# Two ways of turning matrices and of taking a norm's statistics in a graph-network kernel: DMA transposes against 32x32 blocks on VectorE, and bn_stats against two summing passes on ScalarE

## The chip, the cores and the metric

The kernel runs on one core of a Trainium2 chip. The metric is the device time of one execution in microseconds (us), lower is better; where several runs were made, their median is given. All data are 32-bit floats.

## What is computed

The input `x` holds 128 graphs (batch) of 128 nodes with 512 features; `adj` is one 128x128 adjacency matrix that all graphs share. Two residual layers follow each other, each with a layer norm and a relu ahead of it:

```python
# layer 0: graph convolution
h = max(layernorm(x), 0)
deg = adj.sum(axis=1);  d = where(deg > 0, rsqrt(deg), 0)
norm_adj = adj * d[:, None] * d[None, :]
x = x + norm_adj @ (h @ W0) + b0
# layer 1: attention over the graph's edges, 8 heads of 64
h = max(layernorm(x), 0)
q, k, v = h @ Wq + bq, h @ Wk + bk, h @ Wv + bv
scores = q k^T / 8 + (1 - adj) * -1e9
x = x + (softmax(scores) v) @ Wo + bo
```

## The kernel before, in words

**Groups and slots.** The 128 graphs are worked in 32 groups `g` of four (`GB = 4`; graphs b = 0 to 3 of a group, in two halves of two). The work is software-pipelined over time steps `t`, and the order on every engine is the order of the program text: nothing is reordered afterwards. One time step runs five blocks on TensorE: W (the graph convolution's product of group t+1), Q, K and V (the three projections of group t) and Y (the output projection of group t-1). `block` (L1108) runs each as seven steps. Around each step it calls what `plan` has put at a place: the place "Q2" stands ahead of the dense work of step 2 of block Q (`step`, L523), "Q2b" between that and the reads that belong to it (`rest`, L612), "Q2c" behind those. `at(t, place, f, ...)` (L926) fills the plan; the loop from L929 on holds all of it, written out by hand. On one engine an instruction that waits holds up all behind it.

**The products.** From group 1 on each 512-deep product is made by a Winograd-like scheme of seven products (P1 to P7, L31), some of which are split once more in the same way. The operands of the left side lie in a tile of 40 slots of 128 columns (`Operands`, L362: `op_mix` for the convolution, `op_norm` for the normalised and turned h of the attention, `op_att` for the attention's output). Its sums and differences are made by `combine` (L378), mostly on GpSimd. For Q and K the weights are the stationary operand and `op_norm` the moving one (`stay`); for V, W and Y it is the other way round. `halves` (L137) issues each matmul as two of 64 stationary columns. TensorE's results go to PSUM banks a0, a1, b, c, d0, d1; ScalarE makes the first read of a region with the bias (`first`, L785), VectorE adds the later ones (L448, L463). A bank is written again only when its reads are done. In step 1 the product P5 goes to d0 and d1; ScalarE's and VectorE's reads of it stand in `rest` of steps 1 and 2; in step 4 P3 is accumulated onto d1 and then d0. Except in K, the last two pieces of P4 are put off into `tail` and run within steps 1 and 2 of the next block (`left`, L527).

**The turned matrices.** Two things have to be transposed: h ahead of Q, K and V, and the 128x128 attention matrices of the eight heads of each graph (`att`, 128x1024) ahead of `attend` (L890), which stands at V0. For most groups that goes through DRAM. ScalarE splits the 32-bit words into two planes of 16 bits (`split_h` L753, `split_att` L872), the planes are written to DRAM (`write_h` L759, and within `split_att`), and a transposing DMA, which works on 16-bit words here, brings them back turned and interleaved (`turn_h` L762, `turn_att` L878). Groups 0, 1 and 31 have h transposed on TensorE instead (`transpose_h`, as bf16 halves of the words, L742), and some attention matrices at the two ends are too (`turned_in_place` L817, `transpose_att` L881). Five buffers `att_buf` rotate: the turned matrix of graph b lands in the buffer of b-1.

**The norms.** `Norm.statistics` (L331) runs bn_stats and bn_aggr on VectorE for each graph; `scale` (L335) makes 1/sqrt(var + eps) and the negated mean times that on GpSimd; `normalised` (L344) applies both with a relu on ScalarE. The first norm of group t+2 (`ln1`) stands at Q0b, Q1b (half 0) and Q3b (half 1); it is applied (`gcn_norm`) at Q3, Q4, Q5b, Q6 and multiplied with the adjacency matrix on TensorE (`gcn_mix`, tile `pa`) at Q5, Q6, K1, K2. The second norm (`ln2`) of group t+1 stands at K0b and K6b.

**Queues.** All DMAs are issued on SP's queue in program order: reloads of the weights in five parts (`reload_w` L1077), the loads of x two groups ahead, the stores, the planes and the transposing DMAs.

Where the tail is taken up, in `step`:

```python
left = tail.pop(0) if n in (1, 2) and tail else None
...
elif n == 1:
    if inner:
        self.seven(P5, True, (0,))
    ...
    if left:
        left[0]()
    if inner:
        self.seven(P5, True, (1,))
```

Of the kernel before, what the change touches and what calls it, by code (L numbers as in the profile page):

```python
# [8 lines left out]
F32 = mybir.dt.float32  # L9
# [76 lines left out]
def combine_one(engine, t, left, pair, step):  # L86


    def twice(n):
        x, y = (slot_of(left, k, n) for k in pair)  # L90
        return t[:, x : y + 1 : y - x, :]

    out, x, y, minus = step
    engine.tensor_tensor(twice(out), twice(x), twice(y), ALU.subtract if minus else ALU.add)  # L94
# [3 lines left out]
def kernel(  # L98
# [34 lines left out]
    sp = ctx.enter_context(tc.tile_pool(name="sp", bufs=6))  # L133
# [3 lines left out]
    def halves(out, lhsT, rhs, **flags):  # L137

        for y in range(0, P, P // 2):
            nc.tensor.matmul(out[y : y + P // 2], lhsT[:, y : y + P // 2], rhs, **flags)  # L140
# [16 lines left out]
    planes_dram = [dp.tile([P, 2, H * P], U16, tag=f"planes_{b}", name=f"planes_{b}") for b in range(GB)]  # L157
    h_dram = [dp.tile([P, 2, H * P], U16, tag=f"planes_h_{y}", name=f"planes_h_{y}") for y in range(2)]
# [25 lines left out]
    class Weight:  # L184
# [6 lines left out]
        def slot(self, k, n):  # L191
            return self.t[:, slot_of(False, k, n), :]

# [41 lines left out]
    ident16 = const.tile([P, P], BF16, name="ident16")  # L235
# [4 lines left out]
    warm = const.tile([P, 1], F32, name="warm")  # L240

    def constants():
# [5 lines left out]
        nc.gpsimd.tensor_copy(ident16, ident)  # L248
# [41 lines left out]
    def combine_inner(name, engine, steps=range(9)):  # L290
        for k in steps:
            pair, step = INNER[k]
            combine_one(engine, w_sb[name].t, False, pair, step)
# [26 lines left out]
    class Norm:  # L320


        def __init__(self, src, name):
            self.src = src
# [6 lines left out]
        def statistics(self, j):  # L331
            nc.vector.bn_stats(self.st[:, j, :], self.src[:, j, :])
            nc.vector.bn_aggr(self.mv[:, j, :], self.st[:, j, :])

        def scale(self, js):  # L335
            c = slice(js[0], js[-1] + 1)
            nc.gpsimd.tensor_scalar(self.ve[:, c], self.mv[:, c, 1], EPS, None, ALU.add)
            nc.gpsimd.tensor_tensor(self.rs[:, c], self.ve[:, c], mhalf[:, c], ALU.pow)
            for j in js:
# [22 lines left out]
    class Operands:  # L362
        def __init__(self, name):
            self.t = op.tile([P, SLOTS, P], F32, tag=name, name=name)

        def blocks(self, i):
            return self.t[:, LEFT_AT[i] : LEFT_AT[i] + 4, :].rearrange("p (c j) n -> p c j n", c=2)

        def slot(self, i, n):
            return self.t[:, slot_of(True, i, n), :]  # L370

        def blocks_of(self, b):
# [3 lines left out]
            return self.t[:, first + j : first + 8 : 2, :]  # L376

        def combine(self, engine, inner=True, then=None, within=None):  # L378
# [6 lines left out]
            if inner:  # L385
                for step in FIRST_LEFT:
                    combine_one(within, self.t, True, (S1, S4), step)
                for step in WINOGRAD_LEFT:
                    combine_one(within, self.t, True, (A12, A22), step)


    op_mix, op_norm, op_att = (Operands(f"op_{k}") for k in "aho")
    tail = []

    class Projection:
# [13 lines left out]
        def product(self, out, product, fresh):  # L409
# [3 lines left out]
            left, right = self.left.blocks(i), self.right.blocks(k)  # L413
            for c in range(2):
                for r in range(2):
                    start = fresh and c == 0 and r == 0
                    if self.stay:
                        self.matmul(out[:, r], left[:, c], right[:, c, r * P : (r + 1) * P], start)
                    else:
                        self.matmul(out[:, r], left[:, c, r, :], right[:, c, :], start)  # L420
# [224 lines left out]
    def ln1(g, half, js=(0, 1), ready=None):  # L645

        if (g, half) not in scale1:
            scale1[g, half] = Norm(source(g, half), f"1_{g}_{half}")
# [9 lines left out]
    def gcn_mix(g, b):  # L658
# [7 lines left out]
        src = pa.rearrange("p (c n) -> p c n", c=NC)  # L666
        if g == 1 and b < 2:
            nc.vector.tensor_copy(op_a[g].blocks_of(b), src)
        else:
            nc.scalar.copy(op_a[g].blocks_of(b), src)  # L670
# [60 lines left out]
    def transpose_h(g, b):  # L731
# [5 lines left out]
        planes = pt.bitcast(BF16).rearrange("p (z c n) -> p z c n", z=2, c=NC)  # L737
        words = h2.bitcast(BF16).rearrange("n (c f z) -> n z c f", c=NC, z=2)
        for z in range(2):
            for c in range(NC):  # L740
                for y in range(0, P, P // 2):
# [520 lines left out]
```

## Time and profile before

| What | Value |
|---|---|
| median of 3 runs | 2200.97 us (2200.22 to 2202.0) |
| the profiled execution | 2200.75 us, its span from first to last instruction 2199.0 us |
| granted TensorE clock | 0.999 |
| DMA | 595.48 MB, 271 GB/s; its hardware queue's packets took 90.6% of 16 engines' span |
| packets under 512 B | 389,073 of 530,613 |
| transposing DMAs | 121 for att, 58 for h |
| splitting on ScalarE | L875: 121 of 1894 ns; L757: 116 of 1055 ns |
| statistics on VectorE | L332: 144 of 673 ns and 112 of 677 ns; L333: 256 of 182 ns |
| time from issue to landing, median | att planes written 6.3 us, h planes written 3.2 us |

PE is TensorE's matmul row, PEld its weight loads, DVE VectorE, ACT ScalarE, POOL GpSimd, SP the queue that issues the DMAs. In a row of instruction groups there stand the line, the engine, the operation, output and inputs by the program's names, the shapes and the count; then the busy time in us and the mean of one in ns; then the idle time just ahead of them and what ended it. In a timeline the first column is the start in us, the second the length of a run of like instructions, and the bracket at the end gives the idle time ahead and its releaser. In the table by stretch there stand the stretch, its length, the busy time of PE, PEld, DVE, ACT and POOL with their instruction counts, the granted clock, the DMA engines' share and GB/s. A 32-bit matmul appears as two records.

### The profile page before, as it was taken

The numbers are of one execution on the slowest core, as the hardware profiler recorded it, in microseconds if no ns is written. First come the engines' busy times: TensorE is split into PE (matmuls) and PEld (weight loads), VectorE is DVE, ScalarE is ACT, GpSimd is POOL, SyncE is SP. The second block draws the span as 40 slices with busy tenths as digits, with TensorE's granted clock in tenths as the row PEclk, the third lists the DMA queues.
The fourth block names the chain that finished last, engine by engine and source line by source line (L and its number), as shares of the span: only waits on it lengthen the run. The fifth ranks groups of instructions, "written<-read, shape, count | busy, mean of one in ns | idle before, by whom it ended". The sixth has DMA issues, their size and how long they took to land.

```text
span 2199.0 us, 77713 instructions
## 1 busy us (share of the span) xinstructions
PE 2186.2 (99%) x31749; PEld 1879.6 (85%) x31749; DVE 1774.9 (81%) x4244; ACT 1393.8 (63%) x3604; POOL 1886.1 (86%) x2049
## 2 busy tenths in 40 slices
PE   9999999999999999999999999999999999999999
PEld 7788888888888888888888888888888888888887
DVE  7777888878888778888788887788877888878876
ACT  4577665765666666666656676566666565765654
POOL 7988988898889898888988898888889888998754
PEclk9999999999999999999999999999999999999999
DMA  5489999999999999999999999999999999999982
GB/s 165 173 260 289 290 293 292 256 284 307 263 288 287 259 297 280 293 296 244 294 312 262 294 271 269 302 286 276 290 259 289 293 279 298 263 276 298 263 261 84
DMA packets 530613, 595.48 MB, mean 271 GB/s; under 512 B 389073, under 2 KB 396369, under 8 KB 529745
## 3 DMA queue, kind: packets, MB, share of 16 engines
q1 hardware_dynamic: 530256, 590.50, 90.6%
q8 instruction: 251, 4.11, 0.8%
q14 instruction: 106, 0.86, 0.1%
HBM read 358.68 MB, written 137.89 MB: 226 GB/s over the span
## 4 chain that ended last, share of the span: by engine, by line
PE 97%; DVE 1%; issue 0%; POOL 0%; DMA 0%; ACT 0%; SPq 0%; POOLq 0%; DVEq 0%; ACTq 0%
PE bank_a L140 37%; PE bank_d L140 22%; PE bank_b L140 11%; PE bank_c L140 11%; PE pa L140 5%; PE bank_d L831 3%; PE po L901 3%; PE pss L831 1%; PE bank_b L901 1%; PE bank_a L901 1%; PE bank_b L831 1%; PE paT L886 0%; DMA xt<-in_x_dram 0%; DVE xt L448 0%; POOL w L282 0%
## 5 line engine op out<-in xcount | busy, mean ns | idle before, releaser
L858 ACT ACTIVATE att<-att,nmx 128x128 f32<-128x128 f32 x1024 | 396.1, 393 | 0.5 <-DVE nmx L850 0.5
L140 PE MATMUL bank_a<-op_h,w 128*64 128x256 f32 x2976 | 353.5, 380 | 0.0
L870 POOL TENSOR_TENSOR att<-att,rsm 128x1024 f32<-128x1024 f32 x122 | 231.7, 1900 | 110.8 <-DVE rsm L865 98.3
L875 ACT COPY att<-att 128x2048 uint16<-128x2048 uint16 x121 | 229.2, 1894 | 114.6 <-POOL att L870 114.5
L448 DVE TENSOR_TENSOR xt<-xt,bank_d 128x512 f32<-128x512 f32 x610 | 270.3, 468 | 11.0 <-PE bank_d L140 0.5
L140 PEld LDWEIGHTS bank_a<-op_h,w 128*64 128x64 f32 x2976 | 207.9, 137 | 81.6 <-issue 0.5
L140 PE MATMUL bank_d<-op_h,w 128*64 128x128 f32 (+1 forms) x3424 | 221.7, 275 | 0.1
L94 POOL TENSOR_TENSOR op_o<-op_o 128x256 f32<-128x256 f32 x297 | 212.4, 739 | 10.1
L788 ACT ACTIVATE q<-bank_a,bqk 128x256 f32<-128x256 f32 x192 | 79.8, 466 | 211.5 <-PE bank_a L140 211.3
L94 POOL TENSOR_TENSOR op_a<-op_a 128x256 f32<-128x256 f32 x279 | 198.5, 734 | 9.6
L94 POOL TENSOR_TENSOR op_h<-op_h 128x256 f32<-128x256 f32 x270 | 191.2, 733 | 11.5 <-DVE op_h L384 2.1
L140 PEld LDWEIGHTS bank_d<-op_h,w 128*64 128x64 f32 x3424 | 195.0, 137 | 7.1 <-POOL w L282 0.5
L858 ACT ACTIVATION_READ_ACCUMULATOR att<-att,nmx 128x1 f32 x1024 | 196.6, 192 | 0.0
L140 PE MATMUL bank_a<-w,op_o 128*64 128x256 f32 x1536 | 182.2, 379 | 0.0
L140 PE MATMUL bank_a<-w,op_h 128*64 128x256 f32 x1488 | 178.0, 381 | 0.0
L140 PE MATMUL bank_a<-w,op_a 128*64 128x256 f32 x1488 | 176.5, 379 | 0.0
L463 DVE TENSOR_TENSOR xt<-bank_a,xt 128x512 f32<-128x512 f32 x252 | 166.8, 683 | 3.1 <-PE bank_a L140 3.1
L850 DVE TENSOR_REDUCE nmx<-att 128x8 f32<-128x1024 f32 x128 | 154.9, 1210 | 0.0
L356 POOL TENSOR_TENSOR xt<-xt,b_o 128x1024 f32<-128x1024 f32 x62 | 147.2, 2376 | 0.0
L140 PEld LDWEIGHTS bank_a<-w,op_o 128*64 128x64 f32 x1536 | 107.5, 137 | 41.2
L351 ACT ACTIVATE h<-op_o,nb,rs 128x512 f32<-128x512 f32 x112 | 91.8, 820 | 76.2 <-POOL nb L340 76.2
L140 PEld LDWEIGHTS bank_a<-w,op_h 128*64 128x64 f32 x1488 | 102.4, 137 | 43.7
(188 smaller groups left out, 5779.8 us busy)
## 6 DMA issues: line engine op xcount, KB each, us to landing
w<-wd_v SPq DMA_DIRECT2D x155, 512.0 KB, 4.9
w<-wd_o SPq DMA_DIRECT2D x155, 512.0 KB, 9.0
w<-wd_q SPq DMA_DIRECT2D x150, 512.0 KB, 8.3
w<-wd SPq DMA_DIRECT2D x145, 512.0 KB, 5.3
planes<-att SPq DMA_DIRECT2D x121, 512.0 KB, 6.3
out_dram<-xt SPq DMA_DIRECT2D x62, 512.0 KB, 7.4
planes_h<-q SPq DMA_DIRECT2D x58, 512.0 KB, 3.2
op_o<-in_x_dram SPq DMA_DIRECT2D x56, 512.0 KB, 9.8
```

The costliest lines, as they stand in the source:

```text
L94: engine.tensor_tensor(twice(out), twice(x), twice(y), ALU.subtract if minus else ALU.add)
L140: nc.tensor.matmul(out[y : y + P // 2], lhsT[:, y : y + P // 2], rhs, **flags)
L351: nc.scalar.activation(h, src[:, j, :], AF.Relu, bias=nb[:, j : j + 1], scale=rs[:, j : j + 1])
L356: engine.tensor_tensor(t, src, bias.unsqueeze(1).to_broadcast([P, t.shape[1], D]), ALU.add)
L448: nc.vector.tensor_tensor(dst, dst, src, f)
L463: nc.vector.tensor_tensor(t, src.rearrange("p (r f) -> p r f", r=2), t, ALU.add)
L831: nc.tensor.matmul(pss[p][:, c, :], qs[g][rows, c, cols], ks[g][rows, c, cols], start=True, stop=True)
L850: nc.vector.tensor_reduce(nmx, att_of(g, b), AX.X, ALU.max, negate=True)
L858: nc.scalar.activation(att[:, h, :], att[:, h, :], AF.Exp, bias=nmx[:, h : h + 1], scale=1.0, accum_out=sm[:, h : h + 1])
L870: nc.gpsimd.tensor_tensor(att, att, rsm.unsqueeze(2).to_broadcast([P, H, P]), ALU.mult)
L875: nc.scalar.copy(planes, halves)
L901: nc.tensor.matmul(po[p * HD : (p + 1) * HD, c * P : (c + 1) * P], vs[g][:, b, h * HD : (h + 1) * HD], aT[:, p * NC + c, :], start=True, s ...
```

## The change

It has two parts, and edits around them.

**Turning.** VectorE transposes each 32x32 block of the matrix in place of ScalarE's split (`flip_att`, `flip_h`); the blocks are put into one buffer, `spare` (the fifth `att_buf`), which every flip uses, and written to DRAM as 32-bit words. `turn_att` and `turn_h` bring them back with four plain DMAs each (`from_dram`), every one of which fills 32 partitions in runs of 256 words; that puts the blocks in their turned places. The columns come back in four groups of 32. Thus `op_norm` is laid out in quarters (`Operands(..., 4)`): an operand of 128 columns is four pieces of 32 that lie apart. As the moving operand it is read with one more dimension; as the stationary one `halves` issues four matmuls of 32 columns. The turned `att` is read by `attend` with one more dimension. `transpose_h` on TensorE works on whole 32-bit words, without halves.

**Statistics.** For groups above 2 the first norm's `statistics` runs two ScalarE activations with accumulation: a pass that sums to the negated mean, and a pass of squares with that mean as bias. `scale` divides by 512 on the way and makes both graphs' product in one step.

**Around them.** The attention buffers no longer rotate; the places of flips and turns, of `ln2` (Q3b and K0b), of `norm_h` and of some row maxima and exponentials of the first groups change; the combining of group 1's operands goes from VectorE to GpSimd and from W4b to W1b; `sp` has five buffers instead of six. In each triple of the plan's table the first place is for t = 1, the second for the last step, the third for all between.

```diff
     def halves(out, lhsT, rhs, **flags):
-        for y in range(0, P, P // 2):
-            nc.tensor.matmul(out[y : y + P // 2], lhsT[:, y : y + P // 2], rhs, **flags)
+        if len(rhs.shape) == 3:
+            out = out.rearrange("p (q n) -> p q n", n=rhs.shape[-1])
+        elif len(rhs.shape) == 4:
+            out = out.rearrange("p (s q n) -> p s q n", s=rhs.shape[1], q=rhs.shape[2])
+        if len(lhsT.shape) == 3:
+            parts = [lhsT[:, q] for q in range(lhsT.shape[1])]
+        else:
+            parts = [lhsT[:, y : y + P // 2] for y in range(0, P, P // 2)]
+        rows = P // len(parts)
+        for y, part in enumerate(parts):
+            nc.tensor.matmul(out[y * rows : (y + 1) * rows], part, rhs, **flags)
...
+    spare = att_buf[GB].rearrange("p h k -> p (h k)")
...
         def statistics(self, j):
+            if self.summed:
+                src, mv = self.src[:, j, :], self.mv[:, j, :]
+                nc.scalar.activation(unused, src, AF.Identity, bias=0.0, scale=-1.0 / D, accum_out=mv[:, 0:1])
+                nc.scalar.activation(unused, src, AF.Square, bias=mv[:, 0:1], scale=1.0, accum_out=mv[:, 1:2])
+                return
             nc.vector.bn_stats(self.st[:, j, :], self.src[:, j, :])
             nc.vector.bn_aggr(self.mv[:, j, :], self.st[:, j, :])
...
+            if self.summed:
+                nc.gpsimd.tensor_tensor(self.nb[:, c], self.mv[:, c, 0], self.rs[:, c], ALU.mult)
+                return
...
-            scale1[g, half] = Norm(source(g, half), f"1_{g}_{half}")
+            scale1[g, half] = Norm(source(g, half), f"1_{g}_{half}", g > 2)
...
+            self.cut = whole.rearrange("p (q s n) -> p q s n", q=quarters, s=SLOTS)
+
+        def slots(self, some):
+            return self.cut[:, :, some, :] if self.quarters > 1 else self.t[:, some, :]
...
-    op_mix, op_norm, op_att = (Operands(f"op_{k}") for k in "aho")
+    op_mix, op_norm, op_att = (Operands(f"op_{k}", 4 if k == "h" else 1) for k in "aho")
...
-        for z in range(2):
-            for c in range(NC):
-                for y in range(0, P, P // 2):
-                    nc.tensor.transpose(planes[y : y + P // 2, z, c, :], words[:, z, c, y : y + P // 2], ident16)
...
+        for c in range(NC):
+            nc.tensor.transpose(pt[:, c * P : (c + 1) * P], h2[:, c * P : (c + 1) * P], ident)
+        op_h[g].fill(nc.scalar.copy, b, pt)
+
+    def flip_h(g, b):
         half, j = divmod(b, 2)
-        h2 = hs.pop((g, b)).bitcast(U16).rearrange("n (c f z) -> n z c f", c=NC, z=2)
-        planes = h_planes(g, half).rearrange("n (z c j f) -> n z c j f", z=2, c=NC, j=2)
-        nc.scalar.copy(planes[:, :, :, j, :], h2)
...
+        h2 = hs.pop((g, b)).rearrange("n (c i f) -> n c i f", c=NC, i=4)
+        dst = spare.rearrange("n (i c j f) -> n i c j f", i=4, c=NC, j=2)[:, :, :, j, :]
+        nc.vector.transpose(dst.rearrange("n i c f -> n c i f"), h2)
+        if j:
+            nc.sync.dma_start(h_dram[half], spare)
 
     def turn_h(g, half):
...
-        nc.sync.dma_start_transpose(out=blocks, in_=h_dram[half].rearrange("n z f -> (n z) f"))
+        from_dram(op_norm.slots(slice(first, first + 8)).rearrange("f q s n -> f q (s n)"), h_dram[half])
+
+    def from_dram(dst, dram):
+        for i in range(4):
+            part = dram.rearrange("(q f) x -> f q x", q=4)[:, :, i * 256 : (i + 1) * 256]
+            nc.sync.dma_start(dst[i * 32 : (i + 1) * 32], part)
...
-    def split_att(g, b):
...
+    def flip_att(g, b):
+        dst = spare.rearrange("q (i h k) -> q h i k", i=4, h=H)
+        nc.vector.transpose(dst, att_of(g, b).rearrange("q h (i k) -> q h i k", i=4))
+        nc.sync.dma_start(att_dram[b], spare)
 
     def turn_att(g, b):
-        nc.sync.dma_start_transpose(out=att_of(g, b - 1).bitcast(U16), in_=planes_dram[b].rearrange("q z j -> (q z) j"))
+        dst = att_of(g, b).rearrange("k h q -> k (h q)").rearrange("k (q x) -> k q x", q=4)
+        from_dram(dst, att_dram[b])
...
-                ("W1", "-Y6", "W5", turn_att, 0),
-                ("W4b", "-Y6b", "W1b", split_att, 1),
...
-                ("Q4b", "Q0b", "Q3b", split_att, 2),
-                ("Q6b", "Q2", "Q5b", split_att, 3),
...
+                ("W4", "Q0b", "Q0b", flip_att, 0),
+                ("W6", "Q1b", "Q2", turn_att, 0),
+                ("Q3", "Q2", "Q2b", flip_att, 1),
+                ("Q5", "Q3b", "Q4", turn_att, 1),
...
+                ("K1", "Q4", "Q4b", flip_att, 2),
+                ("K3", "Q5b", "Q6", turn_att, 2),
+                ("K3", "Q5", "K0b", flip_att, 3),
+                ("K5", "Q5", "K2b", turn_att, 3),
...
-            at(t, "K0b" if g < NG - 1 else "Q0b", ln2, g, 0)
-            at(t, "K6b" if g < NG - 1 else "Q3b", ln2, g, 1)
+            at(t, "Q3b" if g < NG - 1 else "Q0b", ln2, g, 0)
+            at(t, "K0b" if g < NG - 1 else "Q3b", ln2, g, 1)
...
-                places = ("K6", "K6", "V0b", "V1c", "V1c", "V2", None, None, "Y5")
-                steps = ((norm_h, 0), (norm_h, 1), (norm_h, 2), (norm_h, 3), (split_h, 2), (split_h, 3))
+                places = ("K1c", "K2c", "K4c", "K5b", "K3", "K4b", "K6b", "V0b", "Y5")
+                steps = ((norm_h, 0), (norm_h, 1), (norm_h, 2), (norm_h, 3))
+                steps += tuple((flip_h, b) for b in range(GB))
                 for half in range(2):
-                    at(t, ("V1", "V2b")[half], write_h, g, half)
-                    at(t, ("V5", "Y1b")[half], turn_h, g, half)
+                    at(t, ("V6", "Y1b")[half], turn_h, g, half)
```

## The prediction, made before the changed kernel was run

> **What bounds the kernel now.** I read the page's busy rows and chain of waits first, to see which engine sets the end.
>
> ```profile
> PE 2186.2 (99%) x31749; PEld 1879.6 (85%) x31749; DVE 1774.9 (81%) x4244; ACT 1393.8 (63%) x3604; POOL 1886.1 (86%) x2049
> PE 97%; DVE 1%; issue 0%; POOL 0%; DMA 0%; ACT 0%; SPq 0%; POOLq 0%; DVEq 0%; ACTq 0%
> ```
>
> TensorE carries 97% of the chain: only what lengthens or stops its stream counts. Next, busy time by stretch: the second group of the loop, then one period of the steady loop (score matmuls start every 67.38 us).
>
> ```profile
> 71.20:140.60 69.40, 64.29 (x868) 52.29 (x866) 57.53 (x114) 46.37 (x129) 61.21 (x75) 0.98 0.56 186
> 1016.70:1084.10 67.40, 67.40 (x994) 58.37 (x992) 55.24 (x134) 43.24 (x111) 59.30 (x65) 1.00 0.95 274
> ```
>
> The first PE number equals the stretch in the steady loop: no gap. TensorE stands still for 2.9 us before 71.2, 5.1 us in the second stretch, 4.8 us after 2093. So at most 13 us can be won, and only at the ends; each us of TensorE in the loop costs 30. I then looked for what the change adds there.
>
> **Tiling switches.** `op_norm` becomes four quarters of 32 columns, so where it is the stationary operand (the values projection V) a product is four 128x32 matmuls instead of two 128x64. All else stays 64 wide. The nearest row is a stretch where 128x128 transposes stand between 128x64 matmuls:
>
> ```profile
> 126.44 1.04 PE L140 MATMUL bank_b<-op_h,w 128*64 128x128 f32 x16
> 127.32 0.39 PE L140 MATMUL bank_c<-op_h,w 128*64 128x128 f32 x4
> 127.64 1.09 PE L886 MATMUL paT<-ident,att 128*128 128x128 f32 x8
> 128.66 1.95 PE L140 MATMUL bank_a<-op_h,w 128*64 128x256 f32 x16
> 130.44 0.61 PE L140 MATMUL bank_b<-op_h,w 128*64 128x128 f32 x8
> ```
>
> Sixteen small matmuls take 0.88 us (127.32 - 126.44), so four take 0.22; the transposes start after 0.32 (+0.10). They follow at 0.109 each, eight 0.87, but the next starts after 1.02 (+0.15). The 16 wide ones then take 1.78 where they take 1.73 below (+0.05). Two switches cost 0.30, one 0.15 us. The Trainium skill, TensorEngine Tiling (Array Packing), Key Properties, says that changing the tiling mode, not just the tile, drains the array; it gives no price. By the rule narrowing 64 to 32 columns costs as widening does; without it, nothing. I take the rule with the row's 0.15.
>
> The count: V leaves its last two P4 pieces (`tail`) to steps 1 and 2 of the output projection, between 64-wide matmuls. That is in and out twice, four switches, and one from V's end to the output block; V's entry follows the 64-row scores and pays already. Five by 0.15 is 0.75 us a period, by 30 (t = 1 to 30; group 31 uses undivided operands) **+22.5 us**. Bounds 0 and 32 (0.21, what entering the scores costs). The 12 h transposes of groups 0, 1 and 31 go from 16 bf16 half-width matmuls to 4 of 128x128 f32: 0.45 against 0.44 us, but two switches each: **+3.6 us**.
>
> Does V itself slow down? Twice as many matmuls and weight loads need one pair every 27 ns.
>
> ```profile
> 37.04 0.65 PE L742 MATMUL pt<-ident,att 128*64 128x128 bf16 x16
> 37.49 0.63 PE L140 MATMUL bank_d<-w,op_o 128*64 128x256 f32 x4
> ```
>
> Sixteen pairs pass in 0.45 us, 28 ns each: **0** taken. If the quarters ran only two at a time, V's 10.7 us would double.
>
> **The first norm on ScalarE.** From group 3 on, bn_stats and bn_aggr (0.67 + 0.18 us, four times) leave VectorE. Four times two ScalarE passes come, in Q0b, Q1b (half 0) and Q3b (half 1). A pass is an activation of 512 with an accumulator read. Priced from:
>
> ```profile
> L858 ACT ACTIVATE att<-att,nmx 128x128 f32<-128x128 f32 x1024 | 396.1, 393 | 0.5 <-DVE nmx L850 0.5
> L858 ACT ACTIVATION_READ_ACCUMULATOR att<-att,nmx 128x1 f32 x1024 | 196.6, 192 | 0.0
> L351 ACT ACTIVATE h<-xt,nb,rs 128x512 f32<-128x512 f32 x142 | 113.0, 818 | 12.8 <-POOL nb L340 11.1 <-PE pa L140 1.7
> L850 DVE TENSOR_REDUCE nmx<-att 128x8 f32<-128x1024 f32 x128 | 154.9, 1210 | 0.0
> ```
>
> Exponential pairs start 0.39 us apart in the timeline. ScalarE copies of 1024 and 2048 take 1055 and 1894 ns, 0.82 per element; 384 more give 0.70 a pass. The second pass waits for the first one's mean, about 0.17: 1.57 a block, 3.1 a half. Bounds 2.6 (the 585 ns PSUM copy's spacing) and 3.5 (L351's 0.71). What is queued behind them in Q:
>
> ```profile
> 1055.72 0.84 ACT L788 ACTIVATE q<-bank_a,bqk 128x256 f32<-128x256 f32 x2 [6.75 <-PE bank_a L140]
> 1056.59 0.84 ACT L788 ACTIVATE q<-bank_d,bqk 128x256 f32<-128x256 f32 x2
> ```
> ```profile
> 1059.06 0.42 DVE L448 TENSOR_TENSOR xt<-xt,bank_c 128x256 f32<-128x256 f32 x1
> 1059.39 1.47 DVE L448 TENSOR_TENSOR q<-q,bank_d 128x256 f32<-128x256 f32 x5
> ```
> ```profile
> 1060.72 1.70 PE L140 MATMUL bank_d<-op_h,w 128*64 128x128 f32 x28
> 1062.25 1.04 PE L140 MATMUL pa<-ant,h 128*64 128x128 f32 x16
> 1063.12 1.90 PE L140 MATMUL bank_a<-op_h,w 128*64 128x256 f32 x16
> 1064.85 1.04 PE L140 MATMUL pa<-ant,h 128*64 128x128 f32 x16
> ```
>
> The read of bank_d (1056.59) now stands behind both blocks' passes: 1056.45 + 3.1 + 0.84 = 1060.4. VectorE's five reads follow it (59.39 before), and TensorE needs the third done by 1060.72, the fifth by 1061.37: slack 0.4 to 0.5. A start at 60.45 stops TensorE for 0.7 us. Then ScalarE must still do h0 (mean in at 59.7, GpSimd's three small steps to 61.0, end 61.7), bank_a's read (62.4), half 1's passes (65.6) and h1 (66.4), which the second pa matmul wants at 64.85: **1.5 us late**. That total contains the 0.7.
>
> **The block transposes on VectorE.** The nearest row for 128x1024 is L850, 1.2 us. The Trainium skill (VectorE: DVE Perf Modes, The three transpose paths) has 311 ns for 128 columns; eight such would be 2.5 us, an estimate that pays the start eight times. I take 1.2 (bounds 1.1 and 2.5); for h 0.66. Per period 4 x 1.2 + 4 x 0.66 = 7.4 come and 3.4 leave: 59.2 of 67.4 us, so it is place, not total. At Q2b a flip stands ahead of the five reads; it must wait until the one `spare` buffer has been written out. Flip 0 runs 1054.8 to 1056.0, its write is issued at 1056.1 and lands 3.2 (h planes on the page) to 6.3 us (att planes) later. Near 3.2, as the transposing DMA of that moment is gone: flip 1 then ends at 60.7, the reads start there, TensorE stops 1.1, inside the same 1.5. At 6.3 it is 3.8. The skill's 2.5 would add 1.3. What is late next: the reads end at 62.6, half 0 of the second norm (1.7 us, moved here to Q3b) at 64.3, flip 2, waiting for write 1 till about 64.9, at 66.1, and the read of bank_b at 66.85, wanted by the step-6 matmul at 1065.72 plus the stop so far, 66.9: just in time. Half 1 of that norm moves from K6b to K0b beside flip 3, and the h flips to K3, K4b, K6b, V0b: 0.6 us more than now in a K stage with 4.7 us of VectorE idle: 0; without that cover 0.6 a period.
>
> So **+1.5 us by 29 periods (t = 1 to 29) = 43.5**, bounds 0.4 (2.6 us of passes and a flip that ends early) and 3.8.
>
> **What is hidden.** ScalarE loses 11.8 us of splitting a period and gains 6.3. GpSimd: combining op_h (11.9 us) now has runs of 32; it ends at 1052.8 and is wanted at 1057.5, so up to 38% slower is covered; beyond that each us costs 30. Its chain for the norm loses one 0.27 step. SP's queue: a transposing DMA holds it 3.4 us (median), four plain issues of 0.4 hold it 1.6; the wait for the landed write stays. Packets fall from 389,073 under 512 B to 179 x 512 of 1 KB. Behind it wait the weight reloads, wanted a stage later; if the turn at K2b came late, `attend` would stop TensorE. All 0. The edits for groups 0 and 1 (softmax scale, order, combining) touch the 5.1 us gap: between -5 and +5, taken 0.
>
> **Sum.** The profiled execution took 2200.75 (span 2199.0 and 1.75 around it). + 22.5 + 3.6 + 43.5 = 2270, and the median of the runs is 0.2 from it: **2270**.
>
> **The rivals.** *Switches only* (0.20): passes near 2.6 and a fast flip keep the slack; +26 to +30: 2227 to 2240. For: means on a row are pessimistic where work overlaps. Against: a slack of 0.4. *Spare bound* (0.15): writes land after 6 us, reads start late in every Q, or GpSimd's short runs exceed 38%: +3 to 3.8 us a period, 2313 to 2340. For: 90.6% DMA load. Against: the transposes, 27 of the 90.6 points by the time of the packets under 256 B in the trace, leave for 1 KB packets of half their time. *Faster* (0.08): narrowing needs no drain and both slacks hold, so the loop keeps 67.38; then the earlier norm and combining of group 1 take the 5.1 us gap: 2196. It decides below 0.17 us a period (5.1/30), about one switch. Against: all of the above. *Quarters at half rate* (0.05): 31 x 10.7: about 2530. The main case has 0.52 (2243 to 2312).
>
> **Numbers.** The range takes main case, switches only and spare bound: 2216 to 2335. A measurement of this kernel can tell 0.2% (4.4 us) from no change. Slower 0.92 (0.52 + 0.20 + 0.15 + 0.05), the faster case gives 0.05 faster and 0.03 same.
>
> **What would show it.** Period of the scores: 69.6 (0.75 switches, 1.5 stops). V to output: gaps of 0.2 us where tails stand. New waits: q reads on ScalarE and VectorE in Q, TensorE on bank_d and on h. V's stage still 10.7 us. Wrong if V's length changes, if the period stays under 67.6, or if TensorE stops mainly in K or V0.

## The result and the profile after

The changed kernel takes 2547.93 us (median of 4 runs, 2546.36 to 2550.28), the kernel before 2200.86 beside it: a ratio of 1.1577, 95% interval 1.1557 to 1.1597. The forecast was 2270, with a range to 2335. The direction is right, the size far off: 347 us came where 69 were expected.

The busy row and the chain of waits of the changed kernel:

```profile
PE 2324.5 (91%) x36629; PEld 1909.2 (75%) x36629; DVE 1892.7 (74%) x4247; ACT 1249.0 (49%) x3823; POOL 1866.6 (73%) x1993
PE 55%; DMA 22%; DVE 16%; issue 3%; POOL 2%; ACT 1%; SPq 1%; DVEq 0%; POOLq 0%
```

TensorE has fallen from 97% of the chain to 55; transfers and VectorE have come in. Next, one period from one start of the scores to the next, and within it three stretches from the scores on (columns as in the table by stretch of before):

```profile
1251.25:1329.92 78.67, 72.12 (x1154) 59.51 (x1152) 58.99 (x134) 38.81 (x119) 58.23 (x62) 0.96 0.71 245
1257.80:1261.20 3.40, 2.94 (x20) 2.47 (x24) 2.84 (x6) 0.00 (x0) 3.24 (x4) 0.50 0.40 161
1261.20:1264.60 3.40, 3.40 (x44) 1.71 (x40) 2.36 (x4) 0.06 (x1) 3.32 (x6) 0.54 0.38 154
1264.60:1268.00 3.40, 3.40 (x112) 2.83 (x108) 0.99 (x3) 1.11 (x2) 2.12 (x3) 1.00 0.26 49
```

The period is 78.7 us instead of 67.4; TensorE has 6.5 us without work in it, and for 6.8 us its granted clock is near half (third number from the end). To place the loss I took each stage's length from the first matmul of the stage to the first of the next, as a mean over the 26 periods of t = 3 to 28 (us; t = 0 is the step whose scores start at 71.2 us in the kernel before):

| kernel | scores | V | Y | W | Q | K | attend | period |
|---|---|---|---|---|---|---|---|---|
| before | 3.77 | 10.69 | 11.29 | 11.29 | 13.04 | 13.69 | 3.59 | 67.38 |
| changed | 9.49 | 12.04 | 11.92 | 11.29 | 16.15 | 14.08 | 3.65 | 78.63 |

Half of the loss, 5.7 us, is at the scores, where the prediction had nothing; 3.1 are in Q, 1.35 in V, 0.63 in Y, 0.4 in K (this last was not followed up). Beside these periods, t = 1 alone grew by 21 us (from its scores to the next).

What happens at the scores is read from three timelines. First VectorE:

```profile
1244.50 0.70 DVE L784 STREAM_TRANSPOSE att<-h 128x512 f32<-128x512 f32 x1
...
1256.92 0.71 DVE L784 STREAM_TRANSPOSE att<-h 128x512 f32<-128x512 f32 x1 [7.05 <-DMA turned_h<-att]
1257.55 0.65 DVE L869 SCALAR_TENSOR_TENSOR att<-bank_d,msk 128x512 f32<-128x512 f32 x1
```

The first row is flip 1 of h (K4b); it completes half 0 in `spare`. The second is flip 2 (K6b): it stood idle for 7.05 us, until that half had been written out of `spare`. Behind it waits the first read of the scores (L869). SP's queue shows why the write took so long:

```profile
1244.45 1.38 SPq L1122 DMA_DIRECT2D w<-wd_v  x3
1245.88 2.09 SPq L1122 DMA_DIRECT2D w<-wd_o  x2
1248.06 0.45 SPq L786 DMA_DIRECT2D turned_h<-att  x1
1248.57 1.69 SPq L1122 DMA_DIRECT2D w<-wd_o  x3
```

The write (L786) stands behind five weight reloads of 512 KB. Issued at 1248.06, it let flip 2 start at 1256.92, almost 9 us later. That is typical: over the 26 periods this write landed 9.7 us after its issue (median; 8.6 to 10.8). TensorE meanwhile:

```profile
1253.14 1.06 PE L862 MATMUL pss<-k,q 64*128 64x128 f32 x16
1258.26 2.67 PE L862 MATMUL bank_d<-k,q 64*128 64x128 f32 x16 [4.07 <-DVE att L869]
1260.86 3.60 PE L149 MATMUL bank_a<-w,op_h 128*32 128x256 f32 x32
...
1266.69 1.90 PE L149 MATMUL bank_a<-w,op_h 128*32 128x256 f32 x32
```

The scores of the last graph use banks d0 and d1 a second time and need VectorE's read: a stop of 4.07 us. Then the price of the stop: like runs of 32 matmuls take 3.60 us just after it and 1.90 us six us later. One period earlier a stop of half that length had the same consequence, on TensorE and then in the granted clock:

```profile
1180.59 1.75 PE L862 MATMUL bank_d<-k,q 64*128 64x128 f32 x16 [2.08 <-DVE att L869]
1182.40:1185.80 3.40, 3.40 (x36) 1.70 (x36) 2.84 (x4) 0.00 (x0) 3.32 (x5) 0.50 0.26 101
```

In t = 3 to 28 the granted clock is at half for 167 us in all; in the kernel before, never. The waits over the whole execution (us in total, times, longest) put numbers on both places of the loss:

```profile
DVE att L784 <- DMA turned_h<-att: 211.3, 29, 16.1
PE bank_d L862 <- DVE att L869: 124.3, 29, 11.2
DVE att L907 <- DMA turned<-att: 97.9, 80, 7.7
PE bank_d L149 <- DVE q L490: 63.7, 30, 3.6
```

The last two rows are Q. An example of it, VectorE first and then TensorE:

```profile
1218.98 1.23 DVE L907 STREAM_TRANSPOSE att<-att 128x1024 f32<-128x1024 f32 x1
...
1225.09 1.25 DVE L907 STREAM_TRANSPOSE att<-att 128x1024 f32<-128x1024 f32 x1 [1.53 <-DMA turned<-att]
1226.25 1.44 DVE L490 TENSOR_TENSOR q<-q,bank_d 128x256 f32<-128x256 f32 x5
```
```profile
1227.22 1.75 PE L149 MATMUL bank_d<-op_h,w 128*64 128x128 f32 x28 [2.15 <-DVE q L490]
```

Flip 1 of the attention weights waits for flip 0 to leave `spare` (that write lands after 4.7 us, median of the 26 periods); its five followers, the reads of bank_d, come late, and TensorE stops for 2.15 us. ScalarE's read of bank_d had ended by 1224.5, half a us ahead of the flip's start: in this kernel the sums on ScalarE were not the last to be ready.

### The profile page after: what moved, and what is told of

The parts are those of the page before. It is cut to its first block, busy times and chain, and to the rows that moved or that the text cites. A ratio compares the mean times of both kernels' runs of the same rounds, so it can differ in the third digit from the quotient of the medians.

```text
span 2548.4 us, 88607 instructions
## 1 busy us (share of the span) xinstructions
PE 2324.5 (91%) x36629; PEld 1909.2 (75%) x36629; DVE 1892.7 (74%) x4247; ACT 1249.0 (49%) x3823; POOL 1866.6 (73%) x1993
## 4 chain that ended last, share of the span: by engine, by line
PE 55%; DMA 22%; DVE 16%; issue 3%; POOL 2%; ACT 1%; SPq 1%; DVEq 0%; POOLq 0%
PE bank_a L149 22%; PE bank_d L149 13%; DMA turned<-att 10%; PE bank_b L149 7%; PE bank_c L149 7%; DMA w<-wd_o 6%; DVE xt L490 5%; DMA turned_h<-att 5%; PE bank_d L862 3%; DVE att L907 3%; PE pa L149 2%; DVE xt L505 2%; DVE q L490 2%; DVE k L490 2%; DVE att L869 1%
## 5 line engine op out<-in xcount | busy, mean ns | idle before, releaser
L149 PE MATMUL bank_d<-op_h,w 128*64 128x128 f32 (+1 forms) x3424 | 226.7, 278 | 63.7 <-DVE q L490 63.7
L833 ACT COPY v<-bank_a 128x512 f32<-128x512 f32 x96 | 56.3, 587 | 390.1 <-PE bank_a L149 352.5
L784 DVE STREAM_TRANSPOSE att<-h 128x512 f32<-128x512 f32 x116 | 81.8, 705 | 216.6 <-DMA turned_h<-att 211.3
L907 DVE STREAM_TRANSPOSE att<-att 128x1024 f32<-128x1024 f32 x121 | 150.3, 1242 | 109.1 <-DMA turned<-att 97.9
L862 PE MATMUL bank_d<-k,q 64*128 64x128 f32 x1024 | 114.6, 350 | 125.1 <-DVE att L869 124.3
L149 PE MATMUL bank_a<-w,op_h 128*32 128x256 f32 x2976 | 213.0, 436 | 0.0
L862 PEld LDWEIGHTS bank_d<-k,q 64*128 64x128 f32 x1024 | 96.2, 241 | 140.0 <-DVE att L869 132.2
L149 PEld LDWEIGHTS bank_a<-w,op_h 128*32 128x32 f32 x2976 | 98.9, 125 | 78.8 <-issue 38.9
```

Source lines behind the costliest of these rows:

```text
L149: nc.tensor.matmul(out[y * rows : (y + 1) * rows], part, rhs, **flags)
L784: nc.vector.transpose(dst.rearrange("n i c f -> n c i f"), h2)
L833: nc.scalar.copy(dst, src)
L862: nc.tensor.matmul(pss[p][:, c, :], qs[g][rows, c, cols], ks[g][rows, c, cols], start=True, stop=True)
L907: nc.vector.transpose(dst, att_of(g, b).rearrange("q h (i k) -> q h i k", i=4))
```

## The experiments

The theory after this reading: (a) flip 2 of h waits for a write that is queued behind reloads, and the stop that follows halves TensorE's clock; (b) flip 1 of the attention weights waits for the same buffer in Q; (c) the tile switches cost what was forecast. Rivals: the narrow matmuls are themselves slow (V and Y grew); ScalarE's sums are Q's loss; plain transfers are too slow wherever they are put. Each ratio is to runs of the kernel before made beside it, whose medians lie between 2200.5 and 2202.5 us.

**e1: narrow matmuls alone.** The kernel before; where `op_norm` is stationary, four matmuls of 32 columns.

```diff
-            halves(out, lhsT, rhs, start=start, stop=True, skip_group_check=True)
+            parts = 4 if self.left is op_norm and not self.stay else 2
+            halves(out, lhsT, rhs, parts, start=start, stop=True, skip_group_check=True)
```

> The kernel before with one thing changed: wherever op_norm is the stationary operand (all of V and its two tail pieces in the output projection) a product is four 128x32 matmuls instead of two 128x64; the columns stay contiguous, the result is the same. Theory: only the tile switches cost, 5 a period at 0.15 us, so the time is 2223 to 2240 us, the V stage stays within 0.5 us of its 10.7 us and the output stage grows from 11.3 to 11.9. Rival (narrow matmuls are themselves the loss): V grows by 1.3 us or more as in the changed kernel, and the time is 2255 or more; at half rate about 2530.

Measured: 2223.07 us, ratio 1.0102 (1.0087 to 1.0117): +22.6. V 10.78 us, Y 11.92, all else unchanged. Theory (c) holds; the rival, that narrow matmuls are slow by themselves, falls (what they do beside a pile of reloads comes with e14).

**e2: the sums alone.** The kernel before with the changed `statistics` and `scale` for groups above 2.

> The kernel before with only the first norm's statistics as two summing passes on ScalarE (the st tiles have a pool of their own of 2 buffers to make room for the passes' output). Theory: the block transpose at Q2b, not the sums, holds the five reads in Q of the changed kernel, so alone the sums cost less than the 3.1 us that Q grew by: 0 to 1.5 us a period, 2200 to 2244 us; the q read of bank_d comes some 3 us later than before. Rival (the sums are Q's loss): Q grows from 13.0 to 16 us, 2290 us.

Measured: 2330.28 us, ratio 1.0591 (1.0575 to 1.0607); Q 17.29 us, +4.25. Both forecasts missed low. The timelines of ScalarE and of TensorE in Q say why:

```profile
1198.06 1.89 ACT L888 COPY att<-att 128x2048 uint16<-128x2048 uint16 x1
...
1202.93 0.80 ACT L364 ACTIVATE h<-op_o,nb,rs 128x512 f32<-128x512 f32 x1
```
```profile
1203.78 1.09 PE L141 MATMUL pa<-ant,h 128*64 128x128 f32 x16 [2.41 <-ACT h L364]
```

Here the splits of the attention weights (L888) are still on ScalarE; one of 1.89 us stands ahead of half 1's passes, so the second h is ready that much later than in the changed kernel, where the splits are gone. The slow clock adds to it: it is at half for 51 us in those 26 periods. The run prices the sums beside the splits, not the sums in the changed kernel; that is left to e7, e9 and e10.

**e3: a place of its own for half 0 of h.** The changed kernel; while group 2 is prepared, those columns still hold w_o's last blocks, so that what is saved of w_o has h in it and the output differs by that; the work is the same.

```diff
+        place = spare if half else op_att.t[:, 32:40, :].rearrange("p s n -> p (s n)")
...
-            nc.sync.dma_start(h_dram[half], spare)
+            nc.sync.dma_start(h_dram[half], place)
```

> The changed kernel, but half 0 of the second norm's h is flipped into free columns of op_att instead of the buffer `spare`; half 1 keeps `spare`. So flip 2 at K6b no longer waits until half 0 has been written out. Theory: the score stage falls from 9.5 to 3.8 to 4.5 us, the halved clock after it goes, V loses about 0.8 us: 5.5 to 6.8 us a period less, 2350 to 2390 us. Rivals (narrow matmuls; ScalarE's sums; transfers too slow in general): the score stage stays above 8 us and the time above 2500.

Measured: 2368.09 us (2357.51 to 2370.37), ratio 1.075 (1.072 to 1.078): 180 us less. The score stage is back at 3.77 us, V falls to 11.31, Q stays at 16.07. The gain is in the loop: up to the scores of t = 2 this kernel is only 3.7 us ahead of the changed one (228.5 against 232.2 us).

**e4: no idle clock.** The changed kernel with extra work in the wait.

```diff
+        if b == 2 and 1 <= g < NG - 1:
+            for _ in range(16):
+                nc.tensor.matmul(bank[f"a{turn[0]}"][:, :P], ident[:HD], ident[:HD], start=True, stop=True)
```

> The changed kernel with 16 more matmuls of 64x128 by 64x128 on the identity ahead of the scores of block 2 (groups 1 to 30), whose result is overwritten unread; it adds that work and leaves nothing out. They run while TensorE waits for VectorE at the scores. Theory: the wait stays, but TensorE is not idle for long enough for the granted clock to fall, so the 16 scores take 0.9 instead of 1.7 us and V's first 32 matmuls 1.7 instead of 3.4: 1.0 to 2.4 us a period less, 2475 to 2520 us. If the halved clock costs nothing, the time stays at 2548 or rises by up to 0.9 us a period.

Measured: 2493.28 us, ratio 1.133 (1.1308 to 1.1352): 55 us less with more work. The timeline of TensorE:

```profile
1227.73 3.73 PE L860 MATMUL bank_a<-ident 64*128 64x128 f32 x32
1231.30 1.49 PE L865 MATMUL bank_d<-k,q 64*128 64x128 f32 x16
1232.72 1.93 PE L149 MATMUL bank_a<-w,op_h 128*32 128x256 f32 x32
```

Here the filler takes 3.7 us of the wait, and V's first 32 matmuls then take 1.93 us, as those at full clock do. V falls by 1.0 us, the score stage by 1.2. In t = 3 to 28 the half clock falls from 167 us to 41; it is not gone, since in some periods the filler ends before the wait does. So most of the 1.9 us a period that the run gains (55 by 29) is the clock. Not all of it need be: VectorE's own wait for the half fell too, from 211.3 us to 193.1, or 0.6 a period.

**e5: the write ahead of the reloads.** The changed kernel, one buffer, only SP's order altered.

```diff
-            "W": ((t, "W6"), (t, "Q1"), (t, "K3"), (t, "K3"), (t, "K3")),
-            "Q": ((t, "K4"), (t, "K4"), (t, "K6"), (t, "V0"), (t, "V0")),
+            "W": ((t, "W6"), (t, "Q1"), (t, "K4c"), (t, "K4c"), (t, "K4c")),
+            "Q": ((t, "K4c"), (t, "K4c"), (t, "K6"), (t, "V0"), (t, "V0")),
```

> The changed kernel with only the order on SP's queue altered: the five weight reloads that stand ahead of the write of half 0 (three of w_v at K3, two of w_o at K4) are issued behind it, at the end of K4. The buffer stays shared. Theory: the write is late because it is queued behind 2.5 MB of reloads; now it lands some 4 us after its issue, flip 2 waits 0 to 2 us instead of 7.3, the score stage falls to 3.8 to 6 us: 2360 to 2440 us; more only if w_v itself then comes late for V. Rival (one spare buffer is too slow whatever the order): score stage over 8 us, 2500 or more.

Measured: 2376.99 us, ratio 1.0795 (1.0777 to 1.0813): 171 us less. The score stage is 3.77 us in every period. On SP's queue and then on VectorE:

```profile
1170.95 0.34 SPq L786 DMA_DIRECT2D turned_h<-att  x1
1171.33 1.89 SPq L1122 DMA_DIRECT2D w<-wd_v  x3
```
```profile
1175.51 0.71 DVE L784 STREAM_TRANSPOSE att<-h 128x512 f32<-128x512 f32 x1
```

Issued first, the write is out before flip 2's turn comes: no wait. It now lands after 3.3 us (median) in place of 9.7, though the reloads follow within half a us of it. So the shared buffer and the queue behind the reloads make the wait together; taking away either ends it. Plain transfers are not too slow as such.

**e6: reads first.** The changed kernel with `flip_att` 1 at Q2c instead of Q2b.

> The changed kernel with flip 1 moved from Q2b to Q2c, that is behind the five reads of bank_d on VectorE instead of ahead of them. Theory: the reads start when ScalarE has read bank_d (some 6.6 us into Q instead of 8.4), Q falls by 1.0 to 1.8 us, 2495 to 2520 us; ScalarE's sums hold the rest of Q's loss. If only the sums hold Q: no change, 2540 to 2555. If flip 2 becomes late in turn: little gain, and the K stage longer.

Measured: 2553.55 us, ratio 1.16 (1.1582 to 1.1618): no gain. Q even grew, from 16.15 to 17.14. The waits of TensorE show where it went:

```profile
PE bank_b L149 <- DVE q L490: 58.8, 31, 6.9
PE bank_d L149 <- DVE q L490: 19.0, 29, 3.1
```

Bank_d's wait fell from 63.7 us to 19.0, bank_b's rose from 17.0 to 58.8: the later flip 1 makes its write later, and flip 2 at Q4b waits for that ahead of the reads of bank_b. The move was met by the buffer's next user.

**e7: no sums.** The changed kernel with bn_stats for every group (`g > 2` becomes `False`).

> The changed kernel with the first norm's statistics back on VectorE (bn_stats for every group). Theory: flip 1 with its wait for `spare` still holds the reads of bank_d in Q, so Q falls by less than 0.8 us: 2525 to 2555. Rival (ScalarE's sums are what Q lost): Q falls by 2.5 us or more, 2465 to 2475. The waits at the scores stay.

Measured: 2552.87 us, ratio 1.1592 (1.1563 to 1.162); Q 16.16 us against 16.15. Taking the sums away gains nothing while flip 1 waits for its buffer.

**e8: three mends at once.** e3's place for half 0 (from group 3 on), e6's order, e7's statistics.

> The changed kernel with three mends: half 0 of h is flipped into free columns of op_att (from group 3 on), flip 1 stands behind the five reads (Q2c), and the statistics are back on VectorE. Theory: all that remains is the 0.75 us of tile switches a period, some 0.4 us in K, and the ends: 2225 to 2265 us, with the score stage at 3.8 to 4.5 and Q at 13.0 to 13.8 us. If the plain transfers or VectorE's load are too slow in themselves: 2300 or more.

Measured: 2402.62 us, ratio 1.0918 (1.0902 to 1.0935). The scores are mended (3.77), Q is not (17.06): e6's trap again. The result lies 138 us over the upper end of the forecast, because it took moving a flip for the same as freeing it.

**e9: own places for the flips in Q too.** Flips 1 and 2 of the attention weights and half 0 of h go to three stretches of `op_att` that are free from W to K (att from group 1, h from group 3 on). Order, sums and reloads are the changed kernel's.

```diff
+    def place_of(g, k):
+        free = {1: 8, 2: 24, "h": 32}
+        if g < 1 or k not in free:
+            return spare
+        return op_att.t[:, free[k] : free[k] + 8, :].rearrange("p s n -> p (s n)")
...
-        dst = spare.rearrange("q (i h k) -> q h i k", i=4, h=H)
+        place = place_of(g, b)
+        dst = place.rearrange("q (i h k) -> q h i k", i=4, h=H)
```

> The changed kernel with a place of its own for every flip that follows closely on another: flips 1 and 2 of the attention weights and half 0 of h go into three stretches of op_att's columns that are free from W to K (from group 1, h from group 3 on), flips 0 and 3 and half 1 of h stay in `spare`. Order, sums and reloads are those of the changed kernel. Theory: no flip waits for a write any more; the score stage is back at 3.8 us, and Q keeps only what ScalarE's sums cost beside a flip of 1.2 us, 1 to 2 us a period: 2255 to 2295 us. Rival (the sums alone make Q 16 us long): Q stays at 15.5 to 16.2, 2315 to 2340.

**e10: the same without the sums.**

> The same with the statistics back on VectorE. Theory: Q falls to 13.0 to 13.8 us, since neither the sums nor a wait for a write stands ahead of the five reads of bank_d: 2225 to 2250 us, which is the tile switches and the ends. Rival (VectorE's greater load in Q is a cost of its own): Q over 14.5, 2270 or more.

Measured: 2368.21 us, ratio 1.076 (1.0739 to 1.078), and 2371.76, ratio 1.0761 (1.0738 to 1.0784). The stages, with those of e11 to e14 below (us):

| kernel | scores | V | Y | Q | K | attend | period |
|---|---|---|---|---|---|---|---|
| e9, own places | 3.77 | 12.33 | 12.00 | 14.58 | 13.80 | 4.31 | 72.10 |
| e10, and no sums | 3.78 | 12.24 | 12.00 | 14.62 | 13.81 | 4.68 | 72.42 |
| e11, w_v earlier | 3.79 | 10.78 | 11.92 | 14.59 | 13.96 | 12.14 | 78.48 |
| e12, w_v and w_o earlier | 3.77 | 10.79 | 11.92 | 14.59 | 33.20 | 3.60 | 89.16 |
| e1, narrow, reloads as before | 3.77 | 10.78 | 11.92 | 13.05 | 13.69 | 3.59 | 68.10 |
| e13, wide, reloads late | 3.77 | 10.69 | 11.29 | 13.04 | 13.69 | 3.61 | 67.39 |
| e14, narrow, reloads late | 3.77 | 11.40 | 11.99 | 13.04 | 13.69 | 3.59 | 68.78 |

Q is 14.58 us, the same in every period: 1.54 over the kernel before, no buffer waited for. Both totals missed all the same (2255 to 2295 and 2225 to 2250 were expected), because V and attend grew and t = 1 kept its 21 us (there the flip of h for group 2 still uses `spare`). In Q, VectorE, ScalarE and TensorE of e9 (the second row of TensorE is the second product with the adjacency matrix):

```profile
1215.08 1.24 DVE L915 STREAM_TRANSPOSE op_o<-att 128x1024 f32<-128x1024 f32 x1
1216.24 1.44 DVE L490 TENSOR_TENSOR q<-q,bank_d 128x256 f32<-128x256 f32 x5
```
```profile
1215.31 0.82 ACT L826 ACTIVATE q<-bank_d,bqk 128x256 f32<-128x256 f32 x2
```
```profile
1217.21 1.75 PE L149 MATMUL bank_d<-op_h,w 128*64 128x128 f32 x28 [0.53 <-DVE q L490]
...
1222.13 1.09 PE L149 MATMUL pa<-ant,h 128*64 128x128 f32 x16 [0.57 <-ACT h L374]
```

From the start of Q (1209.56) the bank_d matmul comes at 7.65 us where it came at 6.95 before (1060.72 - 1053.77), 0.70 late, and the second pa at 12.57 where it came at 11.08, 1.49 late. ScalarE's read and the flip end within 0.2 us of each other, so the flip alone would hold the reads nearly as long. e10, with VectorE's statistics in place of the sums, has the same Q: its rival, that VectorE's greater load in Q costs as much by itself, came true. There TensorE waits for VectorE's reads of bank_d and bank_b (16.2 and 16.8 us in all), and no longer for h. At attend, e9's TensorE waits for the turned matrices (12.4 us in 11 waits) and for GpSimd (6.7 us in 7).

**e11 and e12: where V's loss is.** Both are e9 with reloads issued earlier: three of w_v at Q4, Q5, Q6; in e12 the five of w_o also, at K1 and K2. In e12 the last piece of Q's P4, which runs in K2, then stands behind the reload in program order: it multiplies by w_o's columns in place of w_q's and waits for them, so only its V stage says anything.

```diff
-            "W": ((t, "W6"), (t, "Q1"), (t, "K3"), (t, "K3"), (t, "K3")),
+            "W": ((t, "W6"), (t, "Q1"), (t, "Q4"), (t, "Q5"), (t, "Q6")),
```

> The own-buffer kernel (with the sums) with three reloads of w_v moved from K3 to Q4, Q5 and Q6, so that eight reloads no longer leave SP in one go behind the fourth turn. Theory: TensorE's stops inside the V stage, for which the trace names no releaser, come from the V stage running while 4 MB of reloads fill the DMA engines and the narrow matmuls need twice as many instructions; with the pile gone before V begins, V falls from 12.3 us to under 11.5 and attend towards 3.6: 2325 to 2350 us. Rival (the stops have nothing to do with the reloads, but with the narrow matmuls alone): V stays at 12.3, 2360 to 2375. The turns may come later instead: then attend grows.

> The same with the five reloads of w_o moved as well, from K4 to V0 up to K1 and K2, ahead of the fourth turn. Theory: V is free of reload traffic, 10.8 to 11.1 us; but the reads of the fourth turn and the write of half 0 queue behind 2.5 MB, so attend waits for them: 2310 to 2360 us, with attend over 4.3. If V stays at 12.3, the reloads were not its cause.

Measured: 2546.08 us, ratio 1.1561 (1.1544 to 1.1579), and 2873.0, ratio 1.3059 (1.3037 to 1.3081). V is 10.78 and 10.79 us: its stops go with the reloads. (V also starts later here, as attend or K is longer; e13 and e14 part the two causes without that.) Both totals missed, for other places pay. TensorE's wait in e11:

```profile
PE po L945 <- DMA att<-turned: 170.7, 28, 8.0
```

SP issues a turn only when the written blocks have landed, and each write now lands behind a reload: the fourth turn goes out 31 us after Q's start (1252.26 - 1221.31) instead of 25 (1234.59 - 1209.56), and attend waits for it. In this order of the queue, what is issued ahead of a turn delays it.

**e13 and e14: narrow or reloads?** The kernel before, and e1, with the eight reloads held back to some 5 us ahead of the scores, by a DMA of 512 bytes that waits for K's fifth step.

```diff
+    def late(g):
+        nc.sync.dma_start(late_dram, ks[g][0:1, 2, 0:P])
```

> The kernel before (all 64 wide, transposing DMAs) with the eight reloads of w_v and w_o held back to where the own-buffer kernel issues them, some 5 us ahead of the scores, by one more DMA of 512 bytes that waits for K's fifth step. Theory (a pile of reloads stops the narrow matmuls because their instructions come twice as densely): V keeps 10.7 to 10.9 us, 2200 to 2212 us. Rival (the pile stops V whatever the width, or w_v comes late): V grows by 0.8 us or more here too.

> The same with V and its tails as four 128x32 matmuls. Theory: V shows stops without a releaser that it did not show with the reloads in their old place (10.78 us): 11.3 to 12.5 us, and the time is 2240 to 2275. Rival (width plays no part): V as long here as with 64 columns, plus 0.1; 2223 to 2230 if neither stops.

Measured: 2202.92 us, ratio 1.0009 (1.0 to 1.0018), and 2245.64, ratio 1.0203 (1.0188 to 1.0218). Of the four corners only narrow and late stops: V 10.69 (wide, early), 10.69 (wide, late), 10.78 (narrow, early), 11.40 (narrow, late). It takes both. In e9 the stops are those for which the profile names no releaser:

```profile
PE bank_c L149 <- issue: 10.7, 7, 2.4
PE bank_d L149 <- issue: 10.1, 9, 2.0
```

What TensorE waits for there can be read from the trace's DMA packets. One queue of the kind "instruction", q8 on the page, moves packets of 16 KB: 251 in the kernel before and 290 in e1 and e14. By TensorE's records, loads and matmuls together (2 x 31,749 and 2 x 36,773), that is 65 bytes a record in both, so these packets are TensorE's instructions. In V of t = 3 to 28, e14 has 21 places where one record starts over 0.25 us after the one before it. Every one ends 1.26 to 1.55 us after the end of such a packet, while only 7% of V's time lies 1.2 to 1.6 us after one. In e9 all 35 end 1.26 to 1.79 us after one; e1 and e13 have none. They add up to 0.5 us a period in e14 and 1.5 in e9, nearly all that V grew by over e1 (0.6 and 1.55). So the narrow form runs out of instructions when reloads run beside it. The packets in V last no longer in e14 than in e1 (0.86 us on average against 0.94): what makes them come late, and why there are more such stops in e9, no run shows.

## Why the prediction was wrong, point by point

**Tiling switches, +22.5 us: right.** e1 measured +22.6, and V itself at 10.78 us: quarters at half rate was rightly a small rival. The drain that the Trainium skill's TensorEngine Tiling (Array Packing), Key Properties, names without a price is 0.15 us a switch here, if the five switches a period carry all of it. What this term left out is what the narrow form does beside the reloads.

**Sums and flips in Q, 1.5 us: right in size for what it counted.** The two blocks of passes take 3.08 us (1220.62 to 1223.70 in the changed kernel) where 3.1 was taken; e9 shows 0.70 at bank_d and 1.5 in all, the two numbers of the text. Two things were wrong around it. The sums are not its only cause: the flip ends within 0.2 us of ScalarE's read behind them, and without them Q is as long (e10); that the total fits is in part luck. And the wait for `spare` was taken near the 3.2 us landing, "inside the same 1.5"; the write took 4.7 us (median) and Q grew by 3.1, between the two ends that were given (1.5 and 3.8). The landing time came from a kernel whose queue was ordered otherwise. This mis-sized term is 1.6 us a period, some 46 us.

**The h flips, 0: the step that failed.** The text put "the h flips to K3, K4b, K6b, V0b: 0.6 us more than now in a K stage with 4.7 us of VectorE idle: 0; without that cover 0.6 a period". It counted the instructions' busy time and not the wait in one of them. Flip 2 needs the buffer that half 0 is leaving; the write stands behind five reloads; and behind the flip stands VectorE's read of the scores, which TensorE needs. The text saw this pattern for flip 1 of the attention weights and priced it there, and did not ask it again for the other users of the same buffer. The write took 9.7 us, and flip 2 waited 7.3 us on average (211.3 by 29). It cost 5.7 us a period at the scores and 0.7 in V (e3 brings back both): 180 us, and in t = 1 most of 21 more, where TensorE stops for 11.2 us at the scores. That is over half of the miss of 278 us. With Q's 46 it leaves some 30, about what V's further 0.5 us and K's 0.4 make over the loop.

**The clock.** No term of the sum allowed for a stop to cost more than its length. The Trainium skill, TensorE: Matmul & The Clock Gate, HAM oscillation, says that an idle window of about 3.4 us brings the array back to half clock. The trace has the half clock (4.07 us of stop, then 0.50 and 0.54 granted for 6.8 us), but not that length as a bound: 2.08 us of stop were followed by 3.4 us at 0.50 as well. Here the measurement decides: a stop of 2 us can be enough. It need not be: in e9 one of 2.1 us in V (from 603.3) was followed by none. e4 prices it at up to 1.9 us a period, within those 6.4.

**SP's queue, 0: wrong.** The text asked what waits behind the turns. It did not ask what the writes wait behind, and that is what set the 9.7 us (3.3 with the order changed, e5).

**Edits for the first groups, between -5 and +5: right for themselves.** The scores of t = 1 start at 143.4 us against 140.6. The 21 us of t = 1 behind that are the failed step again: its flip 2 waits 16.1 us, the longest of the 29. In e9 one such wait, of 15.7 us in t = 1, is the only one left.

**GpSimd's combining in runs of 32, 0: right.** 731 ns an instruction against 733. The packets that the text calls "under 256 B" are of 256 B; their 27 points are right. The flips' prices were right as well: 1242 ns for 1.2, 705 for 0.66. The text's upper bound of 2.5 for a flip was twice too high. The spare-bound rival (0.15, 2313 to 2340) named the right mechanism, but only for Q, where it cost 1.6 us a period; it did not look at the scores. Two of the text's signs of being wrong came true: V's length changed (12.04 us), and TensorE stops most at the scores, which stand at V0. The text's range, 2216 to 2335, holds no term for such a stop: its own upper bounds for the switches (32) and for Q (3.8 by 29), with the 3.6 of the transposes, end near 2347.

No version here beats the kernel before: its TensorE had no gap in the loop, so the change could only add there. What remains with own places, 72.1 us a period against 67.4, is 0.7 of switches, 1.5 in Q, 1.6 in V, 0.7 at attend and 0.1 in K.

## What to carry to other kernels

When several steps share one staging buffer, each user waits for the previous user's transfer: list all of them in program order, and for each ask where its write stands in the DMA queue and which unrelated work stands behind it on its engine. Price a new stop of the main engine at its length and the slow clock after it: here up to 1.9 us for stops of some 4. Moving a step in such a ring shifted the wait to the next user (e6); in these runs only another buffer or another queue order removed it.

## What the runs showed that was not expected

- A stop of some 4 us on TensorE is followed by up to 6.8 us at half the granted clock, and one of 2.08 us was followed by 3.4; filling the stops with unused matmuls won 55 us without removing the wait.
- 128x32 matmuls of 32-bit data with their weight loads run at full pace on a calm queue (V 10.78 us against 10.69), but stop while 4 MB of reloads run (11.40), and each such stop ends some 1.3 to 1.6 us after a packet of instructions.
- The same write of 512 KB out of the staging buffer lands in 3.3 us when issued just ahead of five reloads of its size (e5) and in 9.7 us when issued just behind them.
